# Edge layer: a shared turn in blocks 0 to 5, ten maxima in block 6, an output and the subtrahends moved into block 6, constant products on TensorE

## The chip, the cores and the metric

The kernel runs on one core of a Trainium2 chip. The metric is the device time of one execution in microseconds (us). The engines are TensorE (PE in the profile; PEld is its weight load), VectorE (DVE), ScalarE (ACT), GpSimd (POOL) and SyncE (SP), which issues most of the DMAs.

## The reference

Four layers with normalizations between them run on four images of 56 x 56 positions with 128 channels. Only layer 1, the edge layer, is changed. For every row of an image, its node features x (56 nodes, 128 channels) give

```python
proj_i = jnp.einsum('blnf,of->blno', x, W1)
proj_j = jnp.einsum('blnf,of->blno', x, W2)
edge = jax.nn.relu(proj_i[:, :, :, None, :] + proj_j[:, :, None, :, :] + be)
edge_sum = edge.sum(axis=3)
node_in = jnp.concatenate([x, edge_sum], axis=-1)
node = jax.nn.relu(jnp.einsum('blnc,oc->blno', node_in, Wn) + bn)
```

with x the group norm of the layer's input, and the result is added to that input. So every node has a ReLU for each of the 56 nodes of its row and for each channel, and their sum.

## The kernel before, in words

**Where it stands.** `build` runs, for each of the four images in turn, layer 0 (`fast_layer`) and then `edge_layer`. The image x1 stays in SBUF as 128 channels x 3136 positions. An image's edge layer begins when layer 0 has written the last of x1, and the next image's layer 0 begins when the edge layer has finished the last of it. After the fourth image comes layer 2 (`spectra`, `attend`, ...), whose weights are loaded by SP (`load_weights`, L158).

**Blocks and turns.** An image is cut into NBLK = 7 blocks of NB = 448 positions (8 rows). In a block, channel o of proj_i + be is laid out as four quarters of 32 channels, each four times over the partitions (tile e_a, 128 x 4 x 448), and minus proj_j as e_pc in PSUM, with a copy e_c in SBUF. Node m of partition group q is node 14 q + m of the row. So one *turn* handles one m of 14, which is four of the 56 nodes: it makes a tile of 128 x 1792, and TensorE sums its partition groups into e_acc with the constant matrix S (L1277: four matmuls, one for each quarter of channels, each in two passes).

**Two kinds of turn.** `EDGE_TURNS = "ddpddpdpddpddp"` (L1147) gives each turn its engine. In a "d" turn VectorE takes max(e_a, -proj_j) (L1222, tile e_td, seven buffers); since max(a, c) = relu(a - c) + c, the sum of the c of the d turns has to be taken off again: VectorE adds them up once in each block (L1290, `rest`), and TensorE takes them off with -S (L1292, "the subtrahends"), after all turns. In a "p" turn GpSimd takes e_a - e_c (L1224, tile e_tp, four buffers) and ScalarE applies the ReLU in place (L1226). In block 0 the first three d turns and the first p turn are made in quarters, as the quarters of e_a arrive.

**The rest of a block.** ScalarE copies e_acc to e_sums (L1295). `output` is two products on TensorE, with the two halves of Wn (L1234, L1235); it is issued for a block at the end of the next one. `finish` (VectorE, L1240) adds max(output, -bn) to x1; it is issued for block j - 2 after turn 3 of block j. `project` (TensorE, L1190 and L1195) makes e_pa and e_pc for block j + 2 at the end of block j, `evacuate` (ScalarE, L1208, L1210, L1212) moves them for block j + 1 after turns 5 and 7, `normed` (ScalarE, L1180; VectorE, L193, for blocks 0 and 1) makes e_xg. After block 6: finish of block 5, then output and finish of block 6. The PSUM tile of `output` has one buffer, so the second output waits for the first finish.

**The order.** Within `tc.manual_schedule` (L1242) TensorE, ScalarE and VectorE run in the order in which the code issues; GpSimd and SP are not in it, and a scheduler places their instructions. All engines work their own instructions off in order.

**The head.** `group_norm_factors` (L2728) stands before that: bn_aggr on VectorE (L2732), a product with g4 on TensorE for the group means (L2734), four small steps on VectorE, a second product for the variances (L2742), a root on ScalarE (L2743) and a reciprocal (L2744). Then e_xg of blocks 0 and 1 (L193), `project(0)`, `evacuate(0)`, and the first maximum.

## Time and profile before

| | us |
|---|---|
| median of 3 runs (3538.6 to 3540.94) | 3538.7 |
| the profiled execution: its time | 3539.16 |
| the profiled execution: its span | 3537.4 |
| TensorE busy, of the span | 3314.4 (94%) |
| VectorE busy | 2706.5 (77%) |
| ScalarE busy | 2101.2 (59%) |
| GpSimd busy | 1252.5 (35%) |
| edge layer of image 1, bn_aggr to the last finish | 546.4 to 689.2 |
| first maximum of images 1 to 4, at | 553.94, 1205.93, 1858.75, 2512.83 |
| end of the last finish of images 1 to 4, at | 689.25, 1341.23, 1994.25, 2648.13 |

How to read it: times are microseconds from the start of the span. A group's line has the code line, the engine, the operation, output <- input, the shape and the count; then busy time in us and mean ns of one instruction; then the idle time of the engine just before them, and what ended most of it. A timeline merges instructions of one kind: start, length, engine, line, operation, shape and count; in brackets the idle time before and what ended it. An instruction's length is longer than the distance to the next one's start, as they are pipelined. A fp32 matmul shows as two passes. The chain of waits follows the work that ended last back through what released it. A table by stretches has, for each, its length, the busy time of PE, PEld, DVE, ACT and POOL with their counts, the granted TensorE clock, the DMA share and GB/s.

### The profile page before, as it was taken

What the parts mean: (1) busy time and instruction counts of PE and PEld (TensorE: products, weight loads), DVE (VectorE), ACT (ScalarE), POOL (GpSimd) and SP (SyncE); (2) the same over time, 40 slices, a digit from 0 to 9 for tenths busy, and PEclk for the clock granted to TensorE, in tenths of its full rate; (3) what the DMA queues carried; (4) which work ended last, traced back from release to release, by engine and by line L of the source; (5) the groups of instructions that cost most, each with busy time, mean ns of one, the idle gap of its engine ahead of it and who ended that gap; (6) DMA issues with size and microseconds to landing.
All of it is one profiled execution on the core that took longest, in us unless ns stands there. A gap on an engine that the chain in (4) does not pass through costs nothing.

```text
span 3537.4 us, 64240 instructions
## 1 busy us (share of the span) xinstructions
PE 3314.4 (94%) x27710; PEld 1425.1 (40%) x27710; DVE 2706.5 (77%) x2566; ACT 2101.2 (59%) x2199; POOL 1252.5 (35%) x764
## 2 busy tenths in 40 slices
PE   6999998889999898999999889999888899999998
PEld 4433333353333434333343443333337443336664
DVE  6588868867888597688859858887795778886776
ACT  4688866558888564788857558887553012214442
POOL 1000007600000491000019400000673778884686
PEclk8999999999999999999999999999998999999999
DMA  2143420014343000444310024442003037753101
GB/s 104 43 93 86 96 52 19 19 48 95 87 92 84 19 1 20 100 95 95 89 45 1 19 61 95 92 98 60 37 14 99 6 70 175 183 139 92 55 19 55
DMA packets 98011, 243.40 MB, mean 69 GB/s; under 512 B 64456, under 2 KB 69832, under 8 KB 92712
## 3 DMA queue, kind: packets, MB, share of 16 engines
q0 software_dynamic: 16128, 102.77, 14.4%
q1 hardware_dynamic: 74872, 123.61, 12.0%
q10 hardware_dynamic: 6720, 12.85, 1.3%
q8 instruction: 219, 3.59, 0.4%
q14 instruction: 72, 0.59, 0.1%
HBM read 79.43 MB, written 31.33 MB: 31 GB/s over the span
## 4 chain that ended last, share of the span: by engine, by line
PE 75%; DVE 15%; ACT 4%; issue 3%; POOL 2%; DMA 0%; DVEq 0%; POOLq 0%; ACTq 0%
PE f_pm L818 18%; PE f_pm L684 15%; PE u_po L1941 8%; DVE e_td L1222 7%; PE e_acc L1277 3%; PE q_acc L1795 3%; PE f_pm L791 2%; PE f_pm L770 2%; PE e_pa L1190 2%; ACT f_ring L821 1%; PE f_pm L464 1%; PE o_d L2204 1%; DVE f_acc L673 1%; PE o_d L2601 1%; PE f_pm L715 1%
## 5 line engine op out<-in xcount | busy, mean ns | idle before, releaser
L821 ACT ACTIVATE f_ring<-f_pm 128x1792 f32<-128x1792 f32 (+1 forms) x764 | 1093.8, 1482 | 229.3 <-PE f_pm L818 181.6
L673 DVE TENSOR_TENSOR f_acc<-f_acc,f_ring 128x1792 f32<-128x1792 f32 x468 | 947.6, 2025 | 191.3 <-ACT f_ring L821 160.2
L818 PE MATMUL f_pm<-f_qT,f_kT 32*128 32x448 f32 x5376 | 725.4, 571 | 15.7 <-ACT f_ring L821 5.1
L684 PE MATMUL f_pm<-f_ring,f_va 128*32 128x448 f32 (+1 forms) x6304 | 589.8, 490 | 0.0
L663 POOL DMA_DIRECT2D f_far<-f_ring x112 | 96.6, 862 | 1333.3 <-ACT f_ring L821 1062.6
L1222 DVE TENSOR_TENSOR e_td<-e_a,e_pc 128x1792 f32<-128x1792 f32 (+1 forms) x288 | 493.1, 1778 | 15.1 <-ACT e_c L1210 15.0
L1224 POOL TENSOR_TENSOR e_tp<-e_a,e_c 128x1792 f32<-128x1792 f32 (+1 forms) x152 | 453.6, 3021 | 74.4 <-issue 42.5
L818 PEld LDWEIGHTS f_pm<-f_qT,f_kT 32*128 32x128 f32 x5376 | 260.0, 183 | 418.0 <-ACT f_ring L821 304.6
L684 PEld LDWEIGHTS f_pm<-f_ring,f_va 128*32 128x32 f32 x6304 | 163.8, 109 | 410.1 <-issue 397.8
L1936 DVE TENSOR_TENSOR u_ud<-u_px,u_d 112x1792 f32<-112x1792 f32 x144 | 263.5, 1863 | 39.6 <-PE u_po L1941 35.4
L1277 PE MATMUL e_acc<-e_td,t_edge 128*32 128x448 f32 x2016 | 225.4, 543 | 42.5 <-DVE e_td L1222 42.3
L1226 ACT ACTIVATE e_tp<-e_tp 128x1792 f32<-128x1792 f32 (+1 forms) x152 | 236.9, 1583 | 44.9 <-POOL e_tp L1224 44.4
L1938 POOL TENSOR_TENSOR u_up<-xh,u_d 112x1792 f32<-112x1792 f32 (+1 forms) x72 | 240.8, 3372 | 55.1 <-PE u_po L1941 41.3
L1941 PE MATMUL u_po<-u_ud,AT 112*64 112x448 f32 x1056 | 213.7, 544 | 1.9 <-DVE u_ud L1936 1.9
L1277 PE MATMUL e_acc<-e_tp,t_edge 128*32 128x448 f32 x1120 | 131.1, 540 | 3.3 <-ACT e_tp L1226 3.3
L1277 PEld LDWEIGHTS e_acc<-e_td,t_edge 128*32 128x32 f32 x2016 | 55.5, 109 | 191.1 <-DVE e_td L1222 116.0
L1941 PEld LDWEIGHTS u_po<-u_ud,AT 112*64 112x64 f32 x1056 | 74.3, 138 | 128.8 <-issue 112.9
L728 DVE RECIPROCAL f_den<-f_den 128x448 f32<-128x448 f32 x28 | 82.6, 2951 | 44.9 <-ACT f_den L725 44.9
L1780 POOL TENSOR_TENSOR q_u<-iS,q_g 128x1792 f32<-128x1792 f32 x32 | 102.8, 3235 | 23.0 <-PE q_acc L1795 23.0
L1795 PE MATMUL q_acc<-q_u,S 64*64 64x448 f32 x1024 | 104.6, 553 | 4.4 <-DVE q_u L1782 3.3
L1941 PE MATMUL u_po<-u_up,AT 112*64 112x448 f32 x480 | 103.9, 546 | 2.4 <-POOL u_up L1938 2.4
L1190 PE MATMUL e_pa<-e_xg,t_edge 128*128 128x448 f32 x224 | 101.0, 577 | 5.1 <-DVE e_xg L193 5.1
(526 smaller groups left out, 4435.6 us busy)
## 6 DMA issues: line engine op xcount, KB each, us to landing
f_far<-f_ring POOLq DMA_DIRECT2D x112, 896.0 KB, 6.3
u_d<-dd SPq DMA_DIRECT2D x46, 784.0 KB
f_far<-f_ring SPq DMA_DIRECT2D x28, 896.0 KB
xw<-in_x SPq DMA_DIRECT2D x4, 1568.0 KB
x2d<-x SPq DMA_DIRECT2D x4, 1568.0 KB
xat<-x SPq DMA_DIRECT2D x4, 1568.0 KB
x_xs<-xat ACTq DMA_DIRECT2D x32, 196.0 KB
xm<-x_ev ACTq DMA_DIRECT2D x64, 98.0 KB
```

What stands on the lines that cost most here:

```text
L673: nc.vector.tensor_add(e.acc, e.acc, slots(j, c))
L684: nc.tensor.matmul(e.po[heads[h], part], va[o, c, heads[h]], p, start=(c == 0), stop=(c == 23 and part.stop == NB))
L818: nc.tensor.matmul(ss[:, i, :NB], kT[heads[h], c * P:(c + 1) * P], qT[heads[h], blk(j)], start=True, stop=True)
L821: nc.scalar.activation(ring[:, slot:slot + m, :], ss[:, :m, :NB], AF.Exp, scale=scale)
L1222: nc.vector.tensor_tensor(t, am, cm, ALU.max)
L1224: nc.gpsimd.tensor_sub(t, am, cm)
L1226: nc.scalar.activation(tf, tf, AF.Relu)
L1277: nc.tensor.matmul(acc[quarters[r0 + r], :NB], w.S[:, 0, :], t[:, r].rearrange("p l n -> p (l n)"), start=(g == 0), stop=False)
L1795: nc.tensor.matmul(acc[bp][i][halves[hb % 2], hb // 2, :NB], x[o], u[o, 8 * hb:8 * hb + 8, :].rearrange("p h t -> p (h t)"), start=first, ...
L1936: nc.vector.tensor_mul(u, bc(px[:, :, :NB], 2, m), dm)
L1938: nc.gpsimd.tensor_mul(u, bc(x, 2, m), dm)
L1941: nc.tensor.matmul(po[64 * b2:64 * b2 + 64, :NB], st.AT[:, 8 * i + h0 + q, 2 * bp + b2, :], u[:, b2, q, :], start=(left == 16), stop=(left ...
```

## The change

- `EDGE_TURNS` becomes `"ddpddpsdpdpddp"` for blocks 0 to 5: eight d, five p and one "s" turn, in place of nine d and five p. In an s turn VectorE takes the maxima of quarters 0 and 1 and GpSimd (with ScalarE's ReLU) the differences of quarters 2 and 3, in half tiles (e_td and e_tp of 128 x 2 x 448, two buffers each). The code for it was there already, unused. `rest` is then made in two reductions.
- Block 6 has its own turns, `EDGE_END = "ddpddpdpdpdddd"`: ten d and four p.
- In block 6, block 5's output is issued after turn 6 and its finish after turn 9; before, both came after block 6's last turn.
- In every block the subtrahends (`rest` with -S) go to TensorE after turn 11 instead of after turn 13. In block 6 the first of the two products of its own output (`begun`) goes there too.
- `group_norm_factors` moves into the manual schedule, and TensorE gets products of two constants (ident and ones, 128 x 384, into an e_pc buffer that nobody reads): two ahead of the product for the means, one behind it, one behind the product for the variances.

The maxima, differences and sums that are computed are the same ones in another split.

```diff
-EDGE_TURNS = "ddpddpdpddpddp"
+EDGE_TURNS, EDGE_END = "ddpddpsdpdpddp", "ddpddpdpdpdddd"
...
-        def output(j, sums):
+        def begun(j):
             po = psum.tile([P, 512], F32, tag="mm", name="e_po")
             nc.tensor.matmul(po[:, :NB], w.Wn[:, 0, :], xg[:, blk(j)], start=True, stop=False)
+            return po
+
+        def output(j, sums, po=None):
+            if po is None:
+                po = begun(j)
             nc.tensor.matmul(po[:, :NB], w.Wn[:, 1, :], sums, start=False, stop=True)
             return po
...
+            idle = psum.tile([P, 512], F32, tag="e_pc", name="e_idle", bufs=2)
+
+            def fill(n):
+
+                for _ in range(n):
+                    nc.tensor.matmul(idle[:, :3 * P], k.ident, bc(k.ones, 1, 3), start=True, stop=True)
+            mr = group_norm_factors(k, wk, bank, st, fill)
...
             for j in range(NBLK):
+                end = j == NBLK - 1
+                turns = EDGE_END if end else EDGE_TURNS
+                nd, ns = turns.count("d"), turns.count("s")
...
                             nc.tensor.matmul(acc[quarters[r0 + r], :NB], w.S[:, 0, :], t[:, r].rearrange("p l n -> p (l n)"),
-                                             start=(g == 0), stop=False)
+                                             start=(g == 0), stop=(g == len(turns) - 1))
...
+                    if g == 6 and end:
+                        po = output(*last)
+                    if g == 9 and end:
+                        finish(j - 1, po)
+                    if g == 11:
+                        for r in range(4):
+                            nc.tensor.matmul(acc[quarters[r], :NB].rearrange("p (l n) -> p l n", l=8), w.S[:, 1, :],
+                                             bc(rest[:, r, :], 2, HH), start=False, stop=False)
+                        if end:
+                            po = begun(j)
...
-                for r in range(4):
-                    nc.tensor.matmul(acc[quarters[r], :NB].rearrange("p (l n) -> p l n", l=8), w.S[:, 1, :],
-                                     bc(rest[:, r, :], 2, HH), start=False, stop=True)
                 sums = wk.tile([P, NB], F32, name="e_sums")
                 nc.scalar.copy(sums, acc[:, :NB])
-                if last:
+                if last and not end:
                     po = output(*last)
                 project(j + 2)
                 last = j, sums
-            finish(NBLK - 2, po)
-            finish(NBLK - 1, output(*last))
+            finish(NBLK - 1, output(*last, po))
...
-def group_norm_factors(k, pool, bank, st):
+def group_norm_factors(k, pool, bank, st, fill):
...
     ps = bank()
+    fill(2)
     nc.tensor.matmul(ps[:, 0:1], k.g4, mv[:, 0:1], start=True, stop=True)
+    fill(1)
...
     nc.tensor.matmul(ps[:, 0:1], k.g4, t, start=True, stop=True)
+    fill(1)
```

More of the change, by code (lines that the diff above doesn't have):

```diff
@@ L1159, in edge_layer @@
     M = HH // 4
-    nd, ns = EDGE_TURNS.count("d"), EDGE_TURNS.count("s")
     quarters = [slice(32 * q, 32 * q + 32) for q in range(4)]
@@ L1168, in bank @@
             return psum.tile([P, 512], F32, tag="mm", name="e_mm")
-        mr = group_norm_factors(k, wk, bank, st)
         xg = big.tile([P, TOK], F32, name="e_xg")
         shift = wk.tile([P, 1], F32, name="e_shift", bufs=1)
-        nc.vector.tensor_scalar(shift, mr[:, 0:1], mr[:, 1:2], -1.0, ALU.mult, ALU.mult)
         ready = {}
@@ L1186, in project @@
             pa = [psum.tile([P, 512], F32, name="e_pa", bufs=4) for r in range(4)]
-            pc = psum.tile([P, 512], F32, name="e_pc", bufs=2)
+            pc = psum.tile([P, 512], F32, tag="e_pc", name="e_pc", bufs=2)
             def first(r):
@@ L1242, in edge_layer @@
         with tc.manual_schedule(engines={mybir.EngineType.PE, mybir.EngineType.Activation, mybir.EngineType.DVE}):
+            idle = psum.tile([P, 512], F32, tag="e_pc", name="e_idle", bufs=2)
[3 more added lines that the diff above has]
+            mr = group_norm_factors(k, wk, bank, st, fill)
+            nc.vector.tensor_scalar(shift, mr[:, 0:1], mr[:, 1:2], -1.0, ALU.mult, ALU.mult)
             for j in range(2):
@@ L1253, in edge_layer @@
                 at, ms = {"d": 0, "p": nd + ns, "s": nd}, []
-                for e in EDGE_TURNS:
+                for e in turns:
                     ms.append(at[e])
@@ L1258, in edge_layer @@
                 if j == 0:
-                    early = {g: tile_of(EDGE_TURNS[g]) for g in
-                             [g for g, e in enumerate(EDGE_TURNS) if e == "d"][:3] + [EDGE_TURNS.index("p")]}
+                    early = {g: tile_of(turns[g]) for g in
+                             [g for g, e in enumerate(turns) if e == "d"][:3] + [turns.index("p")]}
                     for r in range(4):
                         for g, t in early.items():
-                            terms(j, ms[g], t[:, r:r + 1], r, r + 1, EDGE_TURNS[g])
-                for g, e in enumerate(EDGE_TURNS):
+                            terms(j, ms[g], t[:, r:r + 1], r, r + 1, turns[g])
+                for g, e in enumerate(turns):
                     m = ms[g]
```

## The prediction, made before the changed kernel was run

> **What bounds the kernel now.** I went from the page's groups to the waits of VectorE, then to the timelines of VectorE, GpSimd and TensorE in the edge layer of image 1 (span 547 to 689 us), and last to the clock by microsecond. The groups first:

> ```profile
> L1222 DVE TENSOR_TENSOR e_td<-e_a,e_pc 128x1792 f32<-128x1792 f32 (+1 forms) x288 | 493.1, 1778 | 15.1 <-ACT e_c L1210 15.0
> L1224 POOL TENSOR_TENSOR e_tp<-e_a,e_c 128x1792 f32<-128x1792 f32 (+1 forms) x152 | 453.6, 3021 | 74.4 <-issue 42.5
> ```

> VectorE's 288 maxima had 15.1 us of idle time before them in four images, all of it before each image's first maximum. Inside the layer VectorE never waits. Its timeline gives the price of each step:

> ```profile
> 602.19 0.45 DVE L1290 TENSOR_REDUCE e_rest<-e_c 128x32 f32<-128x288 f32 x1
> 602.55 11.66 DVE L1222 TENSOR_TENSOR e_td<-e_a,e_pc 128x1792 f32<-128x1792 f32 x6
> 614.14 0.67 DVE L1240 SCALAR_TENSOR_TENSOR x<-e_po,e_nbn,x 128x448 f32<-128x448 f32 x1
> 614.73 5.87 DVE L1222 TENSOR_TENSOR e_td<-e_a,e_pc 128x1792 f32<-128x1792 f32 x3
> 620.52 0.44 DVE L1290 TENSOR_REDUCE e_rest<-e_c 128x32 f32<-128x288 f32 x1
> ```

> From start to start: a maximum (602.55 to 614.14)/6 = 1.93 us, finish 0.59, the reduction 0.37; a block 620.52 - 602.19 = 18.33. In block 0 fifteen maxima (twelve are quarters) take 553.94 to 566.12, so the twelve take 12.18 - 5.79 = 6.39, 0.53 each. GpSimd has slack in a block, and waits for TensorE to free a tile:

> ```profile
> 619.32 16.14 POOL L1224 TENSOR_TENSOR e_tp<-e_a,e_c 128x1792 f32<-128x1792 f32 x5 [2.19 <-PE e_acc L1277]
> 637.65 16.14 POOL L1224 TENSOR_TENSOR e_tp<-e_a,e_c 128x1792 f32<-128x1792 f32 x5 [2.19 <-PE e_acc L1277]
> ```

> Five differences take 16.1 us, 3.22 each. The four quarters of block 0 take 3.69 together, 0.92 each. Then the layer's tail, in the chain that ended last:

> ```profile
> 681.76 0.04 issue
> 681.81 1.71 PE e_acc L1277 x16
> 683.52 0.75 PE e_acc L1292 x8
> ...
> 686.01 0.69 DVE x L1240
> ...
> 686.75 1.02 PE e_po L1234 x2
> ...
> 688.56 0.04 DVE x L1240
> ```

> The last maximum ends at 681.76 and the last finish at 689.25: 7.49 us, in which two turns, the subtrahends and two outputs go through TensorE one after the other. And its head, where TensorE runs at half clock:

> ```profile
> 549.00:550.00 1.00, 0.18 (x1) 0.18 (x2) 0.96 (x4) 0.00 (x0) 0.00 (x0) 0.86 0.01 0
> 550.00:551.00 1.00, 1.00 (x2) 0.32 (x2) 0.18 (x1) 0.00 (x0) 0.00 (x0) 0.50 0.00 0
> 552.00:553.00 1.00, 1.00 (x32) 0.93 (x20) 0.00 (x0) 0.35 (x1) 0.00 (x0) 0.50 0.00 0
> 553.00:554.00 1.00, 1.00 (x10) 0.49 (x3) 0.06 (x1) 0.53 (x1) 0.00 (x0) 0.93 0.00 0
> ```

> The column before the last two is the granted clock. It falls at about 549.7 and is back at 553.1. From the first maximum to the last finish an image takes 689.25 - 553.94 = 135.3 us, the same in all four. The layer is serial: the next image's first VectorE step starts at 689.16.

> [...] 553.1 - 549.7 = 3.4 us at 0.50. [...] A maximum reads e_pc from PSUM, and costs 1.93 us both beside GpSimd and after it has ended (675.4), so a new balance should slow neither.

> **The change, part by part.**

> *Half tiles.* A half maximum lies on the line through quarter and whole: 0.53 + (1.93 - 0.53)/3 = 1.00 us. A half difference likewise: 0.92 + (3.22 - 0.92)/3 = 1.69; it isn't in the trace, and lies between half a whole (1.61) and two quarters (1.84). The reduction becomes two with the same number of elements: the small VectorE steps start 0.07 us apart at least, so about 0.37 + 0.05 = 0.42.

> *A block 0 to 5.* VectorE: 8 x 1.93 + 1.00 + 0.42 + 0.59 = 17.5 us. GpSimd: 5 x 3.22 + 1.69 = 17.8. TensorE, from its starts in one block (609.26 to 618.21 and on): 14 turns of 0.75, subtrahends 0.86, two output products 0.86 + 0.75, the projections 0.85 + 0.90 + 2.45, in all 17.2; a shared turn has as many products as another. GpSimd becomes the longest; the 18.33 falls by 0.5, not by 0.9.

> *The order on GpSimd.* It isn't written out by hand: in the built kernel the half of blocks 1 to 5 stands ahead of that block's other products, and the half of blocks 3, 4 and 5 even ahead of the last whole product of the block before. That last product closes a block on TensorE, and the output product that VectorE's finish needs (turn 3 of the next block) is queued behind it. So VectorE now waits there, with its maxima queued behind. I follow it, in us after the first maximum. GpSimd never waits, and ends block 4's last product after 3.69 + 24 x 3.22 + 6 x 1.69 = 91.1. ReLU 1.70 and handing over 0.08: 92.9. TensorE's last turn and two products, 0.86 + 0.86 + 0.92: 95.5. VectorE's finish in block 5, the five maxima, the half and the reductions left: 0.59 + 9.65 + 1.00 + 0.42 = 11.7, to 107.2. Block 6: ten maxima, two finishes, a reduction, 19.3 + 1.18 + 0.37 = 20.9, and a wait of 0.4 for block 5's output (VectorE is at it 2.3 us after its fifth maximum, TensorE needs a turn and two products, 2.64): 128.5. Before it was 681.76 - 553.94 = 127.8. VectorE's own work is only 125.0; 3.4 us are waits, so the rebalancing costs 0.7 instead of giving 2.8.

> *The tail.* Block 5's output, its finish, the subtrahends and the first product of block 6 now lie among block 6's turns. Their TensorE work is hidden while VectorE makes the last four maxima (7.7 us against 4 turns and 1.72); without that cover it would be 1.7 us. VectorE's finish is counted above. Left after the last maximum: turn 1.00, copy 0.06 + 0.53, the second product 0.06 + 0.92, finish 0.03 + 0.69 = 3.3 us instead of 7.5. The image takes 128.5 + 3.3 = 131.8 instead of 135.3: 3.5 less.

> *Constant products.* Each is two passes of 128x384. The trace has the same product (L1639): 6 passes in 2.17 us at full clock, 0.32 each, and 8 in 4.84 at half. Two products go ahead of the mean's product; they wait for VectorE and TensorE to be done with the bank (its last reader ends at 545.64) and end at about 547.0, where the mean's product started (546.97): 0.1 us lost. The one behind it is done by 548.0, before 548.15, and the last by 549.2, before 549.82, so they delay nothing else. In the 3.4 us before the fall TensorE had 0.7 us of work; now it has 2.7. While VectorE sets the pace in block 6 it has half (0.96 of 1.93), and the clock stays 1.00. So I take it that it stays. Then the first products take 0.85 + 0.97 instead of 1.79 + 1.69, and the first maximum comes 2.46 us after the first product instead of 4.12, 4.09, 4.22 and 4.02: 6.6 us in four images, less 4 x 0.1 = 6.2. Bounds: 0 if the clock falls anyhow, 5 us lost if the two products run at half clock (2.6 us) ahead of the mean's.

> *After image 4.* On SP the loads of t_w_qk now stand behind x2d and eight small loads, and GpSimd's third memset of s_x, which waited 15.7 us for s_pr, ahead of t_w_qk's first steps. Those steps are 1.4 us, their results are wanted at 2744 (q_u), and GpSimd is idle in between: nothing, within 3 us either way, since TensorE stands still 2.7 us there among these transfers.

> **Sum.** 4 x 3.5 + 6.2 = 20.2 us. The profiled execution took 3539.16 (span 3537.4), so 3519.0; the median of the runs is 0.5 lower: 3518.5.

> **Rivals.** *GpSimd's lag doesn't stop VectorE* (as VectorE has seven tiles of its own to run ahead in): then 2.8 us + 0.7 more in each image, 3504.5. Against it stands the order of finish on VectorE. *The clock falls anyhow*: 3518.5 + 6.2 = 3525; 5 us more if the products come in the way. For it: one window of image 3 at 70% busy did not bring the clock back. *The halves cost two quarters or more*: six of them at 0.15 more, 0.9 us an image, 3522. *Slower*: GpSimd goes on waiting for tiles that TensorE frees, 2.19 us a block as now, since TensorE has only 0.6 us to spare in 17.8. On top of 17.8 that is 6 x 2.19 = 13 us an image, less the 5.1 gained: 3570. It decides from 0.85 us a block. Against it: GpSimd waits now because it runs ahead; a tile comes back within some 3 us of its product, and is wanted 9.7 us after it. That the shared turn isn't done as written can't be: half tiles stand in the built kernel.

> **Numbers.** Forecast with the neighbouring half-tile case 0.72, clock 0.14, no lag 0.09, slower 0.05. Range 3508 (the early halves cost nothing, 1.69 us an image, and halves at 1.61, 2 us in all) to 3528 (the clock falls, and halves at 1.84). What a measurement of this kernel tells from no change is about 0.2%, 7 us, so 3531.6 to 3545.8 is the same: faster 0.91, same 0.05, slower 0.04.

> **What would show it.** Right: GpSimd's maximal gap in blocks 1 to 5 under 0.3 us; VectorE waiting for e_po in finish, 3 to 4 us an image, most in block 3; first maximum to last maximum 128 to 129 us; 3.3 us after it; the clock 1.00 through the head. Wrong: half differences off 1.69, a clock of 0.50 at the head, GpSimd waiting for e_acc, or a stall of TensorE after image 4.

## The result, and the profile after

The changed kernel took 3518.9 us (median of seven runs, 3506.9 to 3530.6), the kernel before 3539.7 on the same chip: ratio 0.9938, interval 0.9917 to 0.9960. The forecast was 3518.5. The profiled execution of the changed kernel took 3527.3 (span 3525.5), 11.9 us less than the one of before. Six later runs had a median of 3507.1; all thirteen lie between 3498.7 and 3532.6, median 3513.6. So this kernel scatters by 34 us, where eleven runs of the kernel before beside the six scattered by 12: the layer has to be read in the trace, and the scatter looked at by itself.

The groups of the page after, which answer to the two of before:

```profile
L1221 POOL TENSOR_TENSOR e_tp<-e_a,e_c 128x1792 f32<-128x1792 f32 (+2 forms) x172 | 480.5, 2857 | 36.7 <-issue 36.7
L1219 DVE TENSOR_TENSOR e_td<-e_a,e_pc 128x1792 f32<-128x1792 f32 (+2 forms) x292 | 478.3, 1703 | 8.8 <-ACT e_c L1207 8.8
```

GpSimd's idle time is now all ahead of each image's first difference (about 9.2 us each; its waits for a tile are gone), and VectorE waits 2.2 us for its first maximum instead of 3.8. The head of image 1's layer, by microsecond, the granted clock again in the column before the last two:

```profile
549.00:550.00 1.00, 0.77 (x3) 0.15 (x2) 0.56 (x3) 0.26 (x1) 0.00 (x0) 1.00 0.24 100
550.00:551.00 1.00, 0.70 (x2) 0.30 (x2) 0.67 (x2) 0.00 (x0) 0.00 (x0) 1.00 0.00 0
552.00:553.00 1.00, 1.00 (x14) 0.49 (x3) 0.15 (x1) 0.53 (x1) 0.05 (x1) 1.00 0.00 0
```

It stays at full clock; the first maximum starts 2.55 us after the first product (2.46 forecast). This is no accident of one execution: in the eleven profiles with the constant products, of the changed kernel and of the experiments below, none of the 44 heads lost the full clock; in the three without them all twelve did. VectorE's timeline, blocks 2 and 3 and then block 6:

```profile
593.98 0.68 DVE L1242 SCALAR_TENSOR_TENSOR x<-e_po,e_nbn,x 128x448 f32<-128x448 f32 x1 [0.96 <-PE e_po L1237]
594.58 4.94 DVE L1219 TENSOR_TENSOR e_td<-e_a,e_pc 128x1792 f32<-128x1792 f32 x3
599.43 0.29 DVE L1312 TENSOR_REDUCE e_rest<-e_c 128x16 f32<-128x144 f32 x1
...
612.98 0.68 DVE L1242 SCALAR_TENSOR_TENSOR x<-e_po,e_nbn,x 128x448 f32<-128x448 f32 x1 [1.48 <-PE e_po L1237]
...
630.77 0.68 DVE L1242 SCALAR_TENSOR_TENSOR x<-e_po,e_nbn,x 128x448 f32<-128x448 f32 x1 [0.26 <-PE e_po L1237]
...
673.29 0.68 DVE L1242 SCALAR_TENSOR_TENSOR x<-e_po,e_nbn,x 128x448 f32<-128x448 f32 x1 [0.42 <-PE e_po L1237]
673.89 7.80 DVE L1219 TENSOR_TENSOR e_td<-e_a,e_pc 128x1792 f32<-128x1792 f32 x4
684.42 0.68 DVE L1242 SCALAR_TENSOR_TENSOR x<-e_po,e_nbn,x 128x448 f32<-128x448 f32 x1 [2.72 <-PE e_po L1237]
```

VectorE never waited in finish inside the layer before; now it does, longest in block 3, for an output product of TensorE (L1237). GpSimd beside it runs without a gap:

```profile
552.95 120.13 POOL L1221 TENSOR_TENSOR e_tp<-e_a,e_c 128x448 f32<-128x448 f32 x43 [9.15 <-issue]
```

And the tail on TensorE, which had 7.5 us of work one after the other:

```profile
680.48 0.96 PE L1290 MATMUL e_acc<-e_td,t_edge 128*32 128x448 f32 x8
681.75 0.96 PE L1290 MATMUL e_acc<-e_td,t_edge 128*32 128x448 f32 x8 [0.31 <-DVE e_td L1219]
683.36 1.02 PE L1237 MATMUL e_po<-e_sums,t_edge 128*128 128x448 f32 x2 [0.65 <-ACT e_sums L1315]
```

One turn and one product are left behind the last maximum: it ends at 681.69, the last finish at 685.10. From the mean's first step on VectorE (bn_aggr) to the last finish an image takes 138.4 us in all four images (142.8 to 143.2 before). Four images: 553.65 instead of 571.69, **18.0 us less**. The profiled executions differ by only 11.9 because other places took longer in this one: the first edge layer starts 0.4 later, the three stretches between layers took 1.1 more, and the stretch from image 4's last finish to the span's end took 894.0 instead of 889.3 us.

### The profile page after: what moved, and what is told of

It is laid out like the page before. It is cut to its first block, busy times and chain, and to the rows that moved or that the text cites. A ratio compares the mean times of both kernels' runs of the same rounds, so it can differ in the third digit from the quotient of the medians.

```text
span 3525.5 us, 64343 instructions
## 1 busy us (share of the span) xinstructions
PE 3329.7 (94%) x27742; PEld 1433.3 (41%) x27742; DVE 2693.9 (76%) x2594; ACT 2118.1 (60%) x2219; POOL 1279.5 (36%) x784
## 5 line engine op out<-in xcount | busy, mean ns | idle before, releaser
L1221 POOL TENSOR_TENSOR e_tp<-e_a,e_c 128x1792 f32<-128x1792 f32 (+2 forms) x172 | 480.5, 2857 | 36.7 <-issue 36.7
L1219 DVE TENSOR_TENSOR e_td<-e_a,e_pc 128x1792 f32<-128x1792 f32 (+2 forms) x292 | 478.3, 1703 | 8.8 <-ACT e_c L1207 8.8
L1223 ACT ACTIVATE e_tp<-e_tp 128x1792 f32<-128x1792 f32 (+2 forms) x172 | 253.4, 1495 | 98.0 <-POOL e_tp L1221 98.0
L1290 PE MATMUL e_acc<-e_td,t_edge 128*32 128x448 f32 x1952 | 231.6, 542 | 6.5 <-DVE e_td L1219 6.1
L1290 PE MATMUL e_acc<-e_tp,t_edge 128*32 128x448 f32 x1184 | 147.9, 543 | 23.7 <-ACT e_tp L1223 23.7
L1290 PEld LDWEIGHTS e_acc<-e_td,t_edge 128*32 128x32 f32 x1952 | 61.7, 110 | 142.5 <-issue 94.4
L804 POOL TENSOR_TENSOR x<-xf,xw 128x343 f32<-128x343 f32 x28 | 25.6, 913 | 225.5 <-DVE xf L793 225.5
```

Source lines behind the costliest of these rows:

```text
L1219: nc.vector.tensor_tensor(t, am, cm, ALU.max)
L1221: nc.gpsimd.tensor_sub(t, am, cm)
L1223: nc.scalar.activation(tf, tf, AF.Relu)
L1290: nc.tensor.matmul(acc[quarters[r0 + r], :NB], w.S[:, 0, :], t[:, r].rearrange("p l n -> p (l n)"), start=(g == 0), stop=(g == len(turns) ...
```

## Experiments

All twelve, with the layer (bn_aggr to last finish, four images, against before), the stretch behind image 4 in the profile, and the whole time. Each ratio is to runs of the kernel before on the same chip. x_again to x_oldturns ran on one chip, x_calm, x_notail, x_whole and x_both on another, the last four on a third, so whole times are compared within these groups.

| run | layer, us | stretch behind | median (lowest to highest) | ratio, interval |
|---|---|---|---|---|
| before | 0.0 | 889.3 | 3539.7 (3536.8 to 3542.0) | 1 |
| changed | -18.0 | 894.0 | 3518.9 (3506.9 to 3530.6) | 0.9938, 0.9917 to 0.9960 |
| x_again | -18.0 | 903.6 | 3507.1 (3498.7 to 3532.6) | 0.9911, 0.9896 to 0.9926 |
| x_order | -23.4 | 883.6 | 3508.2 (3500.3 to 3531.2) | 0.9920, 0.9895 to 0.9945 |
| x_nofill | -9.9 | 882.5 | 3519.7 (3508.8 to 3525.4) | 0.9946, 0.9932 to 0.9959 |
| x_oldturns | -14.2 | 890.1 | 3524.9 (3521.1 to 3527.2) | 0.9961, 0.9948 to 0.9974 |
| x_notail | -0.6 | 878.7 | 3526.6 (3522.8 to 3531.0) | 0.9963, 0.9950 to 0.9976 |
| x_whole | -29.9 | 892.5 | 3509.2 (3506.3 to 3512.2) | 0.9907, 0.9894 to 0.9920 |
| x_calm | -18.1 | 875.1 | 3514.8 (3507.2 to 3548.7) | 0.9941, 0.9918 to 0.9964 |
| x_both | -32.0 | 902.2 | 3520.7 (3499.2 to 3523.8) | 0.9927, 0.9906 to 0.9948 |
| x_calm2 | -18.0 | 886.8 | 3523.8 (3518.0 to 3525.2) | 0.9943, 0.9930 to 0.9956 |
| x_base2 | +0.1 | 885.9 | 3538.9 (3532.7 to 3541.3) | 0.9989, 0.9981 to 0.9997 |
| x_both2 | -32.0 | 874.8 | 3506.7 (3493.7 to 3518.4) | 0.9908, 0.9893 to 0.9924 |
| x_fin6 | -19.6 | 880.9 | 3516.3 (3509.8 to 3526.3) | 0.9935, 0.9921 to 0.9949 |

**x_again**, nothing edited.

> The changed kernel as it is, once more, for its scatter (3506.9 to 3530.6 in seven runs, where the kernel before has 5 us). Theory: the edge layer takes the same time in every execution (first maximum to last finish 132.2 to 132.3 us in image 1, within 0.1 us of the first profile), and what differs lies outside it, in windows of 3.41 us at half clock that fall on different stretches after the layer: a stretch bound by TensorE loses up to 1.7 us for each. Then a slower execution has a lower granted clock. Rival: the layer itself varies, because VectorE's waits for TensorE come out differently from run to run; then the layer's length differs by some us between the two profiles of this kernel. Median 3519, between 3507 and 3531 for a single run.

First maximum to last finish was 132.28 us (132.25 in the first profile), the waits in finish 0.97, 1.48, 0.25, 0.27, 0.43: the layer repeats itself. The profiled execution had the granted clock 0.980 and took 3532.6; the one at 0.990 took 3498.7. So the theory held, but not its size: the median was 3507.1 instead of 3519, and four of the six runs lie outside 3507 to 3531. What brings the clock down is asked in x_calm to x_both2.

**x_order**

```
-        with tc.manual_schedule(engines={mybir.EngineType.PE, mybir.EngineType.Activation, mybir.EngineType.DVE}):
+        with tc.manual_schedule(engines={mybir.EngineType.PE, mybir.EngineType.Activation, mybir.EngineType.DVE,
+                                         mybir.EngineType.Pool}):
```

> The changed kernel with GpSimd's differences in the written order (the half stands at its turn, no longer ahead of the products of its block and of the block before). Nothing else moves on any engine. Theory of the prediction: the early halves delay each block's last whole product by 1.69 us, TensorE's output product is queued behind that, and VectorE waits for it in finish: without them the waits in finish fall from 0.96, 1.48, 0.26, 0.26 to 0.4 at most each, the last maximum ends 127.4 us after the first instead of 128.8, first maximum to last finish 130.7 to 130.9 instead of 132.25: 1.4 us an image, 5.6 us in all, 3513. Rival: VectorE waits because GpSimd has more work in a block (17.8 us) than VectorE (17.5), in whatever order: 132.2 and 3519 as now. GpSimd itself ends after 120.1 us in both.

The same five finishes in VectorE's timeline:

```profile
595.77 0.68 DVE L1242 SCALAR_TENSOR_TENSOR x<-e_po,e_nbn,x 128x448 f32<-128x448 f32 x1 [0.50 <-PE e_po L1237]
...
613.57 0.68 DVE L1242 SCALAR_TENSOR_TENSOR x<-e_po,e_nbn,x 128x448 f32<-128x448 f32 x1 [0.26 <-PE e_po L1237]
...
631.37 0.68 DVE L1242 SCALAR_TENSOR_TENSOR x<-e_po,e_nbn,x 128x448 f32<-128x448 f32 x1 [0.27 <-PE e_po L1237]
```

The wait of block 3 fell from 1.48 to 0.26, first maximum to last finish from 132.25 to 130.96, with GpSimd's run 120.15 us as it was (120.13). That of block 2 fell from 0.96 to 0.50 only (0.4 at most was expected). So the early halves cost 1.3 us an image; the order, not the amount of GpSimd's work, makes this part. The layer's 5.4 us are not visible in the whole time (3508.2 beside 3507.1): the scatter is larger.

**x_nofill**

```
-            idle = psum.tile([P, 512], F32, tag="e_pc", name="e_idle", bufs=2)
...
-                for _ in range(n):
-                    nc.tensor.matmul(idle[:, :3 * P], k.ident, bc(k.ones, 1, 3), start=True, stop=True)
+                return
```

> The changed kernel without the constant products. Theory: the clock falls to 0.50 at the head of each image's layer again, the first maximum comes 4.0 us after the first product instead of 2.55, the mean's copy 0.1 us sooner: 1.4 to 1.5 us more an image, 5.8 us in all, 3525. From the first maximum on nothing changes (132.2). Rival: the head is faster because the windows lie elsewhere now that the program runs shorter, not because of the products: the clock stays at 1.00 without them too in some images, and the time is 3519 or, without the 0.1 us, a little less.

The clock column at its head:

```profile
552.00:553.00 1.00, 0.76 (x1) 0.50 (x2) 0.61 (x2) 0.00 (x0) 0.00 (x0) 0.50 0.00 0
555.00:556.00 1.00, 1.00 (x18) 0.67 (x10) 0.00 (x0) 0.18 (x1) 0.00 (x0) 0.50 0.00 0
556.00:557.00 1.00, 1.00 (x3) 0.41 (x2) 0.61 (x2) 0.35 (x1) 0.52 (x1) 0.68 0.00 0
```

The half clock is back in all four images, and 4.15 us from the first product to the first maximum with it, so the rival falls. It cost more than 1.5 us an image: 140.55, 140.76, 139.89, 140.56 against 138.4. In images 1, 2 and 4 two windows fell at half clock (549.8 to 556.6 here), the later quarters came late, GpSimd started late (a gap of 0.48 us after its first quarter), and the wait of block 2 grew from 0.96 to 1.41; that nothing would change after the first maximum was wrong. The products are worth 2.0 us an image, 8.1 in all.

**x_oldturns**

```
-EDGE_TURNS, EDGE_END = "ddpddpsdpdpddp", "ddpddpdpdpdddd"
+EDGE_TURNS, EDGE_END = "ddpddpdpddpddp", "ddpddpdpddpddp"
```

> The changed kernel with the turns of before in all seven blocks (nine maxima, five differences, no shared turn), the tail's moves and the constant products kept. Theory: the new turns bring little, since what GpSimd takes over comes back as VectorE's waits: the last maximum ends 128.4 us after the first (127.8 as before and a wait of some 0.6 for block 5's output in block 6), and the last turn is a difference, so 4.5 us are left behind it instead of 3.4: 132.9 instead of 132.25, 2.6 us more in all, 3521. No wait in finish in blocks 2 to 5, GpSimd waits 2.2 us a block for tiles as before. Rival A: the rebalancing is worth its full 2.8 us an image: 135.0, 3530. Rival B: it costs 0.7 us, as a sum against the kernel before says: 131.6, 3516.

GpSimd's timeline has the old waits again:

```profile
616.91 16.14 POOL L1221 TENSOR_TENSOR e_tp<-e_a,e_c 128x1792 f32<-128x1792 f32 x5 [2.19 <-PE e_acc L1290]
635.24 16.14 POOL L1221 TENSOR_TENSOR e_tp<-e_a,e_c 128x1792 f32<-128x1792 f32 x5 [2.19 <-PE e_acc L1290]
```

VectorE waits in no finish before the last; the last maximum ends 128.41 us after the first (128.4 expected), with 4.82 us behind it (4.5 expected): 133.22 instead of 132.25. The 128.4 came true for another reason than the expected one: no wait of 0.6 stands in block 6, but block 5's finish (0.59) now lies among the maxima (127.81 + 0.59). So with the tail moved, the new turns give 1.0 us an image: they end the maxima 0.4 later, and leave 1.4 less behind them because the last turn is VectorE's.

**x_notail**

```
...
-                    if g == 6 and end:
-                        po = output(*last)
-                    if g == 9 and end:
-                        finish(j - 1, po)
-                    if g == 11:
...
+                for r in range(4):
+                    nc.tensor.matmul(acc[quarters[r], :NB].rearrange("p (l n) -> p l n", l=8), w.S[:, 1, :],
+                                     bc(rest[:, r, :], 2, HH), start=False, stop=True)
                 sums = wk.tile([P, NB], F32, name="e_sums")
                 nc.scalar.copy(sums, acc[:, :NB])
-                if last and not end:
+                if last:
                     po = output(*last)
...
-            finish(NBLK - 1, output(*last, po))
+            finish(NBLK - 2, po)
+            finish(NBLK - 1, output(*last))
```

> The changed kernel with the tail of before: block 5's output, its finish, the subtrahends and the first output product of block 6 stand behind block 6's last turn again. Turns and constant products stay. Theory: the last maximum ends at 128.7 to 128.9 us as now (no finish in block 6, but no wait of 0.42 for block 5's output either; a third of a us less at most), and behind it come a turn, the subtrahends, two outputs and two finishes, 6.3 to 6.7 us instead of 3.4 (before: 7.5 with a difference as the last turn): 135.3 us from the first maximum to the last finish instead of 132.25, 12 us more in all, 3525 to 3531. Rival: the moved products delay TensorE's turns in block 6 by what they save at the end; then 132.5 to 133.

Last maximum after 128.49; behind it 7.44 us in image 1 (6.3 to 6.7 expected), 9.37 in image 2, 7.48 in image 3 and 8.39 in image 4. TensorE's timeline in image 2, and two stretches of 3.4 us there, before and after 1330.6:

```profile
1328.12 0.96 PE L1290 MATMUL e_acc<-e_td,t_edge 128*32 128x448 f32 x8 [0.97 <-DVE e_td L1219]
1330.05 1.24 PE L1290 MATMUL e_acc<-e_td,t_edge 128*32 128x448 f32 x8 [0.97 <-DVE e_td L1219]
1331.98 1.72 PE L1290 MATMUL e_acc<-e_td,t_edge 128*32 128x448 f32 x8 [0.69 <-DVE e_td L1219]
1333.47 1.72 PE L1305 MATMUL e_acc<-e_rest,t_edge 128*32 128x448 f32 x8
...
1327.20:1330.60 3.40, 1.51 (x16) 0.31 (x16) 3.40 (x3) 0.00 (x0) 0.00 (x0) 1.00 0.00 0
1330.60:1334.00 3.40, 2.71 (x20) 0.59 (x16) 1.32 (x1) 0.00 (x0) 0.00 (x0) 0.50 0.00 0
```

A turn goes from 0.96 to 1.72 us: the clock fell to 0.50 from 1330.6 to 1337.4. Between the last four maxima TensorE is busy less than half the time (1.51 of 3.40 us), and without the moved products the clock fell there in all four images, in images 1 and 3 too (one window of 3.41 us each, from 678.6 and from 1982.5). In image 1 one turn is wholly behind the last maximum, and it takes 1.48 us to the next product's start instead of 0.76; without this the 7.44 would be some 6.7, as expected. With 6.7 in every image, an estimate from image 1's timeline, the half clock cost 5.8 us in the four tails (32.7 - 4 x 6.72).

The move is worth 17.4 us in four images (571.08 - 553.65), nearly all that the change gives, and by this estimate a third of it is that it keeps the clock up. The kernel before did not need that: its block 6 has two maxima at the most between differences, no window of the tail fell to half clock, and TensorE was busy 55% or more in each window of block 6. In the changed kernel TensorE is busy 67% or more in each window of 3.41 us across the last four maxima, in all four images, and the clock is 1.00 there. So the four maxima at the end of the new turns are where the clock can be lost, and the moved products hold it. The parts don't add up to 18.0 (17.4 + 8.1 + 3.8), because each is taken out of the whole: without the tail's moves, turns and products together give 0.6.

**x_fin6**

```
-                    if g == 3 and po is not None:
+                    if g == 6 and po is not None:
```

> The changed kernel with finish after turn 6 instead of turn 3 in every block, GpSimd's order left as it is. Theory: VectorE isn't held by where finish stands but by TensorE, which works its turns in order and is itself held by GpSimd's last product of the block before; with finish later VectorE runs three maxima further and then waits for a tile of its seven, or in finish again: the waits inside blocks 2 to 5 get a little shorter, not gone, first maximum to last finish 132.0 us (132.25 now). Rival: finish stands too early, and that alone makes VectorE wait: the 3 us of waits in blocks 2 to 5 go, and 129.3 us are left.

131.88. The waits in blocks 2 to 4 are gone, and one of 2.94 us stands before the second finish of block 6:

```profile
670.52 0.47 DVE L1313 TENSOR_REDUCE e_rest<-e_c 128x32 f32<-128x320 f32 x1
673.94 0.68 DVE L1242 SCALAR_TENSOR_TENSOR x<-e_po,e_nbn,x 128x448 f32<-128x448 f32 x1 [2.94 <-PE e_po L1237]
674.54 7.80 DVE L1219 TENSOR_TENSOR e_td<-e_a,e_pc 128x1792 f32<-128x1792 f32 x4
```

VectorE runs ahead and meets TensorE at the next place where it needs a product. So the waits of blocks 2 to 4 went, as the rival said, and without its gain: the sum was as the theory had it (132.0), at another place (no wait for a tile).

**x_whole**

```
-EDGE_TURNS, EDGE_END = "ddpddpsdpdpddp", "ddpddpdpdpdddd"
+EDGE_BLOCKS = ("ddpddpdpddpddp", "ddpddpdpdpdpdp") * 2 + ("ddpddpdpddpddp",) * 3
-                turns = EDGE_END if end else EDGE_TURNS
+                turns = EDGE_BLOCKS[j]
```

and the edits of x_order and x_fin6.

> The changed kernel without half tiles: blocks 1 and 3 have eight maxima and six differences, the other five blocks nine and five, in written order on GpSimd, with finish after turn 6 instead of turn 3. GpSimd makes 37 whole differences, where the shared turns make 34 and a half, VectorE 61. Theory: what kept the rebalancing from paying was the place of GpSimd's last product in every block, not the half tile's size: with GpSimd ahead in blocks 0, 2, 4, 5 and 6 VectorE never waits in finish but once, the last maximum ends after 124.8 us, first maximum to last finish 129.4 (a difference is the last turn, so 4.8 are left): 2.9 us an image less than the changed kernel, 11 in all, 3496 to 3507. Rival: six differences make a block of 19.4 us on GpSimd, longer than any other; VectorE waits for it in blocks 2 and 4, 1.5 us each: 132.3, nothing gained.

The expectation miscounts: the changed kernel's GpSimd makes 37 differences too (6 x 5.5 + 4), and VectorE 61 maxima (6 x 8.5 + 10). So the same work is split in the same shares, only by whole turns of single blocks, and VectorE no longer waits in any finish but the last:

```profile
614.68 0.68 DVE L1242 SCALAR_TENSOR_TENSOR x<-e_po,e_nbn,x 128x448 f32<-128x448 f32 x1
...
631.04 0.68 DVE L1242 SCALAR_TENSOR_TENSOR x<-e_po,e_nbn,x 128x448 f32<-128x448 f32 x1
...
672.52 0.68 DVE L1242 SCALAR_TENSOR_TENSOR x<-e_po,e_nbn,x 128x448 f32<-128x448 f32 x1
```

Last maximum after 124.47, 4.82 behind it, 129.29: 2.96 us less than the changed kernel, GpSimd's run as long as ever (119.7). So it was not how much GpSimd has to do that held the changed kernel back, but what stands where. Three things were moved at once here (the turns, GpSimd's order, finish); alone the order gave 1.3 us and finish 0.4, and how the rest divides was not run.

**x_calm, x_both**

```
-        apply_norm(k, x[:, t:t + 14, :], x[:, t:t + 14, :], mr)
+        if b == B - 1:
+            nc.scalar.activation(x[:, t:t + 14, :], x[:, t:t + 14, :], AF.Identity, bias=sh, scale=mr[:, 1:2])
+        else:
+            apply_norm(k, x[:, t:t + 14, :], x[:, t:t + 14, :], mr)
```

(`sh` is minus mean times factor, a new 128x1 tile.) x_both also has shared turns in blocks 0 to 4, the old turns in blocks 5 and 6, and the edits of x_order and x_fin6.

> The changed kernel; only the normalization of image 4 after its edge layer (four instructions of 128x784) is made on ScalarE instead of VectorE. It is for the scatter of the whole time (3498.7 to 3532.6 in 13 runs), which isn't in the edge layer: two profiles of the same kernel agree there within 0.1 us in every image. Theory: in that stretch GpSimd works without a gap on weights of the next layer, and VectorE's four instructions, 0.68 us each in images 1 to 3, took 14.2 us together in one profile of the changed kernel, 13.8 in the next, 6.2 in the variant in written order, 12.1 in the kernel before, as they happen to meet GpSimd's. On ScalarE they take about 0.8 us each whatever GpSimd does: the stretch from the end of the layer to the span's end becomes 884 us or less (894.0 and 903.6 in the two profiles, 883.6 in the variant where they met least), and the scatter falls to about that of the kernel before (11.6 us) : 3500, in a band of 10 to 14 us. Rival: the scatter comes from the half-clock windows alone; then it stays at 24 to 34 us and the median at 3507 to 3519.

> A faster version, if the theories hold: shared turns in blocks 0 to 4 only, nine maxima and five differences in blocks 5 and 6, written order on GpSimd, finish after turn 6, and image 4's normalization on ScalarE. Theory: first maximum to last finish 128.9 us (last maximum 124.2, 4.8 behind it) instead of 132.25: 13.4 us in four images, and the stretch after image 4 as in the run with ScalarE's normalization alone: 3487, in a band of 10 to 14 us. Rival: GpSimd, which now has 121.8 us without a gap, ends too late for the last turns: 131 in the layer, 3495.

VectorE's timeline in the changed kernel's first profile, behind image 4:

```profile
2665.95 4.73 DVE L193 TENSOR_SCALAR x<-x,s_mr 128x784 f32<-128x784 f32 x1
2670.61 0.62 DVE L1594 TENSOR_TENSOR s_z<-s_pr,norm 128x462 f32<-128x462 f32 x1
2671.16 8.70 DVE L193 TENSOR_SCALAR x<-x,s_mr 128x784 f32<-128x784 f32 x2
```

In x_calm's profile these are on ScalarE and the stretch is 875.1 us, the shortest so far. But ten of its runs lie between 3507 and 3522, two at 3546.7 and 3548.7: the scatter did not fall, so the expectation failed. The granted clocks side with its rival: 0.976 in the two slow runs, 0.983 to 0.988 in the ten. As the clock in the profiles is either 1.00 or 0.50 (all 44 records before and all 44 after), a run's time at half clock can be estimated from its clock (twice what is missing to 1, times its time): 170 us in the two, 84 to 120 in the ten. Over the twelve the whole time goes with it, about 0.5 us for each us at half clock (correlation 0.99; in x_again's six runs 0.985). This says what the scatter consists of, not what brings the clock down.

x_both missed its forecast (3520.7 instead of 3487). Its profile shows a part of it. Its layer is as forecast (128.77), and yet the stretch took 902.2, because the next instruction of the kind now stood still:

```profile
2653.50 0.49 DVE L1580 RECIPROCAL s_d<-s_d 128x56 f32<-128x56 f32 x1
2654.03 12.89 DVE L1581 TENSOR_SCALAR norm<-s_d,t_images 128x56 f32<-128x56 f32 x1
2663.34 3.58 DVE L232 COPY xh<-s_px 112x448 f32<-112x448 f32 x1
```

A scaling of 128x56, 0.3 us in the kernel before, lasts 12.89, from 2654.03 to 2666.9, while GpSimd goes from one operation to the next, and TensorE waits 8.5 us for what VectorE makes after it. Against x_both2, in which this scaling is on ScalarE, TensorE's same products come 16.2 us later from 58 us behind the layer on; 10 us more are lost some 600 and 730 us behind it, where two more stretches of half clock stand and VectorE's scaling has long been done.

**x_calm2, x_base2, x_both2**: the same edit and this scaling on ScalarE too, in the changed kernel, the kernel before and the version of x_both.

```
-    nc.vector.tensor_scalar_mul(st.norm[:, b, 1, :], d, w.ng[:, 0:1])
+    if b == B - 1:
+        nc.scalar.activation(st.norm[:, b, 1, :], d, AF.Identity, scale=w.ng[:, 0:1])
+    else:
+        nc.vector.tensor_scalar_mul(st.norm[:, b, 1, :], d, w.ng[:, 0:1])
```

> The changed kernel with image 4's normalization on ScalarE as in the run before, and with it the one small scaling (128x56) after it, which took 12.9 us on VectorE in one profile (2654.0 to 2666.9, GpSimd busy without a gap), 1.5 in another and 0.3 in the kernel before. Theory: VectorE's instructions with one source, from SBUF to SBUF, stand still while GpSimd works back to back, for as long as chance has it; with the five largest on ScalarE the stretch after image 4 is 875 to 880 us in the profile, and nearly all executions lie within 15 us, around 3506: none at 3546 as two of twelve with the normalization alone on ScalarE. Rival: the half-clock windows are the cause and VectorE's long instructions only coincide: the scatter stays at 25 to 40 us.

> The kernel before, with the same five instructions on ScalarE and nothing else changed. Theory: VectorE's four long instructions (12.1 us in its profile, 2.7 without the delay) give back some 10 to 13 us: 3527. The difference to the changed kernel with the same edit is then the change itself without the noise of that stretch: 18 to 20 us by the edge layer's own times (142.9 us from the mean's step to the last finish before, 138.4 after, four images: 18). Rival: the kernel before doesn't suffer there, its scatter being small (14 us in 17 runs): 3539 as ever, and the gain of the changed kernel is 30 us or more in this comparison.

> A faster version: shared turns in blocks 0 to 4 only, nine maxima and five differences in blocks 5 and 6, written order on GpSimd, finish after turn 6, and the five instructions of image 4's normalization on ScalarE. The layer took 128.8 us from first maximum to last finish with these turns (132.25 in the changed kernel). Theory: four times 3.5 us less than the changed kernel with the same five instructions on ScalarE: 3492, within 15 us in nearly all executions. Rival: what the layer gives is lost behind it again, 3505 to 3520.

Half of it came true. In these profiles no instruction of VectorE in the 75 us behind the layer takes over 1.7 us, and x_calm2's five runs lie within 7 us; but at 3523.8, not 3506. Its stretch was 886.8, and the clock says why. By four microseconds, from 2653 on:

```profile
2653.00:2657.00 4.00, 2.91 (x7) 2.03 (x8) 2.23 (x10) 1.14 (x4) 1.45 (x6) 0.54 0.70 198
2657.00:2661.00 4.00, 4.00 (x58) 2.96 (x58) 0.79 (x4) 2.05 (x5) 1.99 (x8) 0.50 1.01 408
2661.00:2665.00 4.00, 2.79 (x14) 1.11 (x10) 2.39 (x4) 2.71 (x5) 3.90 (x5) 0.50 0.87 351
2665.00:2669.00 4.00, 3.43 (x34) 3.23 (x35) 1.20 (x5) 0.07 (x1) 3.90 (x7) 0.50 0.01 5
2669.00:2673.00 4.00, 4.00 (x49) 3.94 (x48) 0.64 (x1) 0.81 (x2) 4.00 (x6) 0.50 0.01 2
```

TensorE, the first pair after the comma, works 70 to 100% of these stretches, and the clock stays at 0.50 for 20.5 us (2653.3 to 2673.7); in x_calm and x_both2 it was 1.00 in the same stretch, and their products were 9.1 to 9.2 us ahead at the end of it. So the rival has its part: with no standing VectorE at all, the half clock goes with 9 us here. x_base2 stayed at 3538.9, as its rival said: 3.2 us below the kernel before on the same chip (3542.1), though the 12.1 us of its four normalizations were off VectorE. So there they held up little. x_calm2 is 15 us below x_base2, where the layer gives 18.0. x_both2's layer kept its 128.8; its runs of 3493.7 to 3518.4 are 17 us below x_calm2 on the same chip, of which the layer's turns are 14.0; at 3506.7 they are not the forecast 3492 but in their rival's range. Over the fourteen profiles the two longest stretches behind the layer (902.2 and 903.6) have the most half clock in them, 79 and 81 us, the two shortest (874.8 and 875.1) only 32 and 35. What decides in an execution whether the clock falls in that stretch, and why the kernel before scatters less, stays open.

## Why the prediction was right

**Its mechanism and most terms held.** GpSimd never waits for a tile (0.01 us a layer, under 0.3 forecast) and ends after 120.2 us: 33 wholes, four quarters and six halves at the forecast 3.22, 0.92 and 1.69 make 120.1. That a new balance slows neither engine was, for GpSimd, the author's estimate (measured was VectorE's 1.93 us beside GpSimd and without it), and it held: a whole difference takes 3.22 us from start to start before and after, a whole maximum 1.93. VectorE waits in finish for 3.4 us an image before the last, 1.48 of them in block 3 (3 to 4, most in block 3). The clock stays at 1.00 through the head. x_order shows the reason that was only argued: with the halves at their turn, the waits of blocks 2 and 3 fall from 0.96 and 1.48 to 0.50 and 0.26.

**The sum was 2.2 us too high for the layer**: 18.0 instead of 20.2. Three terms: the last maximum ends 128.85 us after the first instead of 128.5 (1.2 in four images, against before's 127.8); 3.41 us behind it instead of 3.3 (0.5); the head gives 5.8 instead of 6.2 (0.4, as the first product to the first maximum is 2.55 to 2.63, not 2.46).

**The split was less right than the sum.** "The rebalancing costs 0.7 instead of giving 2.8" puts block 5's finish (0.59), which the tail's moves bring in among the maxima, to the account of the turns. x_oldturns has that finish and the old turns, and takes 1.0 us more an image: the new turns gain, because the last one is VectorE's. And the constant products, taken out, cost 8.1 us, not 6.2: 1.8 of them fall after the first maximum, where a late start goes on to the wait of block 2. A small sum is off too: the terms named for the range's low end (1.69 us in four images, and 2 us) lead to 3509.7, not to 3508.

**Where a step was too small.** "Nothing, within 3 us either way" was said of what comes after image 4. The stretch there took 874.8 to 903.6 us in the profiles, 894.0 and 903.6 for the very same kernel. The edit's own share in it can't be told from this noise. So it is luck that the median came within 0.4 us of 3518.5: the layer's 18.0 alone, taken from 3539.7, give 3521.7; the thirteen runs have 3513.6, and single runs left the range 3508 to 3528 on both sides.

**The argument for the clock was too simple.** "While VectorE sets the pace in block 6 it has half, and the clock stays 1.00" served to say that half the time busy is enough; and that 2.7 us of work in 3.4, instead of 0.7, hold the clock was the author's estimate. In the kernel before, differences stand between the maxima, and no window of 3.41 us in block 6 had under 55%; at the four heads the products made it 82 to 88%, so the forecast came true without this argument. Where TensorE really had less than half, in x_notail (1.51 of 3.40), the clock fell. And in x_calm2 it stayed at 0.50 for 20.5 us, four of its six windows busy throughout. How far a busy share tells what the clock will do is worked out in the last section.

**The rivals.** That the lag wouldn't stop VectorE: the waits stand in the timeline. That the clock falls anyhow (1.00 at the head), that halves cost as much as two quarters (1.68 us from start to start, where two quarters are 1.84), that GpSimd goes on waiting for tiles (0.01 us a layer): each is refuted by the profile after.

## What to carry to other kernels

When two engines feed a third that works in written order, balance is not enough: the last piece of a block should come from the engine that is ahead, or everything behind it in the order waits (1.48 us in block 3 here, 0.26 in x_order). Take serial work at the end of a stage and put it between the last steps of the engine that sets the pace; here that was worth more (17.4 us in four images) than the new turns (3.8), and kept TensorE's clock at 1.00, where it fell to 0.50 without it (x_notail). Where a kernel scatters by more than the change, measure the stage's own span in the trace, and profile the same kernel twice to learn which stages repeat themselves.
